# A filter's odd-frequency interpolation, started by half a channel in place of a whole one

## The chip, the cores and the metric

The kernel runs on one NeuronCore of a Trainium2 chip. The core has five engines that each work through their own list of instructions: TensorE (matrix products), VectorE, ScalarE and GpSimd (element by element), and SyncE, which here mostly issues DMA transfers, in order ("SP" in the profile). They meet through semaphores. Sixteen DMA engines move data between HBM and the core's memory. The metric is the time on the device, in microseconds: the median of three runs. In single precision a product of 128 x 512 takes more than one pass, so the profile shows several matmul instructions for one in the code.

## The reference, cut to what matters

Two layers; the change lies in the filter of the first. `x` is (4, 512, 512, 16): four images, 16 channels in, 16 out.

```python
def _L0_conv_ref(x, h0, numerators, denumerator):
    l1, l2 = 512, 512
    a = jnp.pad(denumerator, ((0, 0), (0, 0), (1, 0), (1, 0)), constant_values=1.0)
    b = jnp.pad(numerators, ((0, 0), (0, 0), (0, 0), (1, 0), (1, 0)), constant_values=0.0)
    H_truncated = jnp.fft.rfft2(b, s=(l1, l2)) / jnp.fft.rfft2(a, s=(l1, l2))
    h_truncated = jnp.fft.irfft2(H_truncated, s=(l1, l2))
    H_full = h0 + jnp.fft.rfft2(h_truncated, s=(2 * l1, 2 * l2))[0]
    X = jnp.fft.rfft2(x, s=(2 * l1, 2 * l2), axes=(-3, -2))
    Y = jnp.einsum('...hwi,ijhw->...hwj', X, H_full)
    return jnp.fft.irfft2(Y, s=(2 * l1, 2 * l2), axes=(-3, -2))[..., :l1, :l2, :]

x = x + _L0_conv_ref(_gn(x), L0_conv_h0, L0_conv_numerators, L0_conv_denumerator)
x = x + _L1_conv_ref(_gn(x), L1_conv_kernel, L1_conv_bias, L1_conv_radius)
```

For each pair of an input and an output channel, the filter is a quotient of two polynomials at 512 x 512 frequencies. It is brought back to 512 x 512 taps and transformed again at twice the length, so it is needed at the old frequencies along the second axis (the even ones of the long transform) and at those between them (the odd ones).

## The kernel before, in words

Four stages follow one another: the filter, the forward transform of the images, the product with the filter and the way back along one axis, and the last stage with the second layer. TensorE runs a stage's instructions after those of the stage before it. The change lies in the filter stage, `filter_phase`.

**The pairs.** The list `work` holds 512 entries: output channel `j` (16), half `kp` of the first axis's frequencies (2), half `h` of the even second-axis frequencies (2), and two input channels `i`, `i + 1` (8 steps). For a channel that is 32 entries, 16 for each `kp`. An entry goes through three passes of the main loop (line 490), so one pass works on three entries at different stages: `polynomials` (line 357, TensorE) evaluates numerator and denominator; `evict`, `products`, `terms` and `quotient` divide on ScalarE, VectorE and GpSimd (lines 368 to 393; the reciprocal is line 392); `taps` (line 410, TensorE) goes back along the first axis and `placed` (line 421, ScalarE) puts the outcome into the staged tiles `st`. With the last entry of a `(j, kp, h)` four DMAs (line 428) store the tiles into `g_d[h]`: two halves `a` of the 128 rows, and in each two groups `q` of 16 rows, at row 64 a + 32 q + 16 kp. A half `kp` therefore fills four groups of 16 rows, and columns that belong to channel `j` alone.

**The interpolation.** `odd(j)` makes the odd frequencies of channel `j` from the even ones: 16 blocks `tb`, each of four rows in two places. A block is loaded by four DMAs of 256 KB (`ev_in`, line 448; two buffers, the next block is asked for one block ahead), multiplied by the constant `todd` (line 462), copied by ScalarE to `ot` (line 467), and stored by four DMAs of 256 KB into `g_d[2]` and `g_d[3]` (line 468). It is a generator: it yields four times in a block, after the two products that fill one PSUM tile. What lies between two yields is called a unit here. A channel has 64 units, the kernel 1024.

**How the two are interleaved.** `odds()` runs through the channels and holds each back until `done[0]` has reached 64 (j + 1) + 8; `done[0]` grows by 2 with each finished entry of `work`. A pass of the loop asks the generator twice (lines 493 and 506), so at most two units run in a pass. After the loop, line 521 adds 8 and what is left of the interpolation runs on its own (line 522), with nothing beside it.

**The order.** `InOrder` fixes the order of the instructions of TensorE, VectorE, ScalarE and GpSimd inside the loop to that of the program. SyncE's list of DMAs isn't fixed in this way: its order is made by the framework's planner from what is ready. The queue itself works in order, so a DMA that waits holds back those behind it. The statistics of the images for the next stage run in the same loop on VectorE (`beside`, line 586).

Of the kernel before, what the change touches and what calls it, by code (L numbers as in the profile page):

```python
# [49 lines left out]
C = 16  # L50
# [150 lines left out]
def dram(t, row, offset, *dims):  # L201

    pitch = t.shape[1]
    lead = [[pitch, t.shape[0]]] if row is None else []
    return bass.AP(tensor=t.tensor, offset=t.offset + (row or 0) * pitch + offset,
                   ap=lead + [list(d) for d in dims])
# [28 lines left out]
def filter_phase(tc, cst, h0, num, den, g_d, beside):  # L235
    nc = tc.nc
    with ExitStack() as ctx:
# [193 lines left out]
                            in_=st[a].rearrange("p (q r e) i -> p q r (e i)", q=2, e=8)[:, q],  # L431
                        )

        def odd(j):

            def place(tb):
                first = ((0, 96), (64, 32))[tb // 8]
                return [(first[c] + 4 * (tb % 8)) * GP + j * 8 * C for c in range(2)]  # L440

            step = [GP, 4], [1, 8 * C]

            def load(tb):
                ev = evp.tile([P, 2, 2, 32 * C], F32, name="ev_in")
                for h in range(2):
                    for c in range(2):
                        nc.sync.dma_start(
                            out=ev[:, h, c].rearrange("p (s e) -> p s e", s=4),
                            in_=dram(g_d[h], None, place(tb)[c], *step),  # L450
                        )
                return ev

            ev = load(0)
            for tb in range(16):
                after = load(tb + 1) if tb < 15 else None
                for hh in range(2):
                    ot = odp.tile([P, 2, 32 * C], F32, name=f"ot{hh}")
                    for c in range(2):
                        pt = ps_t.tile([P, 32 * C], F32, name="pt", tag="t")  # L460
                        for kc in range(2):
                            nc.tensor.matmul(  # L462
                                pt, todd[:, c, kc, hh * P : hh * P + P], ev[:, kc, c],
                                start=(kc == 0), stop=(kc == 1),
                            )
                        yield
                        nc.scalar.copy(ot[:, c], pt)
                        nc.sync.dma_start(
                            out=dram(g_d[2 + hh], None, place(tb)[c], *step),
                            in_=ot[:, c].rearrange("p (s e) -> p s e", s=4),  # L470
                        )
                ev = after

        def odds():

            for j in range(C):
                while done[0] < 64 * (j + 1) + 8:
                    yield
                yield from odd(j)

        work = [dict(j=j, h=h, i=i, kp=kp)
                for j in range(C) for kp in range(2) for h in range(2) for i in range(0, C, 2)]
        done, us = [0], {}
        order = InOrder(tc, nc.tensor, nc.vector, nc.scalar, nc.gpsimd)
        rest = odds()
        for _ in weights(0):
            pass
        quad(0, 0, 0)
        coming = iter(())
        for p in range(len(work) + 2):  # L490
            new, mid, last = (work[p - k] if 0 <= p - k < len(work) else None for k in range(3))
            with order:
# [18 lines left out]
                j, kp, r = p // 32, p // 16 % 2, p % 16  # L511
# [952 lines left out]
```

## Time and profile before

| | |
|---|---|
| time before, median of three runs | 16199.08 us (16192.73 to 16224.64) |
| the profiled execution's own time | 16219.56 us |
| its span, first to last instruction | 16217.8 us |
| filter stage, to the end of line 462 | about 3776 us |
| of it, line 462 on TensorE | 4096 instructions, 1924.9 us busy, from 291.0 us on |
| line 392, reciprocal on VectorE | 1024 instructions, 1722.9 us busy |
| mean granted TensorE clock | 0.969 of full speed |

The span is one execution, a little slower than the median of the runs; shares and durations are read from it. Busy time of TensorE is modelled: matmuls overlap in the array, so the time from one start to the next is a better measure of what one costs than its mean duration. A share of busy time is only told for the stretch that it was taken over, since the stages have different limits. In an order of time, a figure in brackets is idle time of the engine before the instruction, with what ended it.

### The profile page before, as it was taken

How to read it: one execution, taken by the hardware profiler on the slowest of the kernel's cores; microseconds unless marked ns; L12 is line 12 of the kernel's file. 1: busy time of each engine (PE TensorE's matmuls, PEld its weight loads, DVE VectorE, ACT ScalarE, POOL GpSimd, SP SyncE). 2: the span in 40 equal slices, each digit the busy share in tenths (PEclk: the TensorE clock that was granted, in tenths of full speed). 3: DMA queues.
4: the chain of work that ended last, by engine and by line, in shares of the span. 5: the costliest groups of instructions: out<-in, count | busy, mean ns of one | idle time of the engine just before them, and what ended most of it. 6: DMA issues, size and time to landing. Idle time of an engine off the chain costs nothing. (4 is left out here: it accounts for less than half of the span.)

```text
span 16217.8 us, 539020 instructions
## 1 busy us (share of the span) xinstructions
PE 14720.9 (91%) x232588; PEld 10874.5 (67%) x232588; DVE 10679.6 (66%) x21019; ACT 8839.0 (55%) x17007; POOL 10556.5 (65%) x10157
## 2 busy tenths in 40 slices
PE   7999999999988888888888888888888889888898
PEld 5555555554557666667676676677676767777787
DVE  8999999993545555555555555555555555778877
ACT  4666666663345555555555555555555553147788
POOL 7777777772356666666666666666666665667766
PEclk8999999999999999999999999999999999989899
DMA  4888888888878888888888888888888888975521
GB/s 138 239 244 246 244 245 239 244 242 259 251 271 329 326 330 329 330 329 326 329 327 328 330 327 329 326 324 330 329 329 330 328 330 305 326 253 196 197 103 66
DMA packets 2917339, 4542.72 MB, mean 280 GB/s; under 512 B 125730, under 2 KB 2094076, under 8 KB 2805262
## 3 DMA queue, kind: packets, MB, share of 16 engines
q1 hardware_dynamic: 2705758, 3836.11, 68.6%
q0 software_dynamic: 172336, 605.00, 9.4%
q10 hardware_dynamic: 36864, 67.13, 1.2%
q8 instruction: 1830, 29.98, 0.7%
q14 instruction: 551, 4.51, 0.1%
HBM read 3030.45 MB, written 1477.31 MB: 278 GB/s over the span
## 5 line engine op out<-in xcount | busy, mean ns | idle before, releaser
L848 PEld LDWEIGHTS pm<-xe,gh 128*32 128x32 f32 x131328 | 1996.9, 111 | 1437.8 <-issue 1141.2
L848 PE MATMUL pm<-xe,gh 128*32 128x64 f32 x131328 | 2366.9, 222 | 649.6 <-issue 320.2
L832 PE MATMUL pg<-c_dg,g 64*128 64x128 f32 x32832 | 2607.1, 290 | 311.9 <-ACT gh L732 195.8
L877 DVE TENSOR_TENSOR z<-zq,pz 128x256 f32<-128x256 f32 x2052 | 860.0, 419 | 2956.7 <-ACT zq L876 2952.5
L832 PEld LDWEIGHTS pg<-c_dg,g 64*128 64x128 f32 x32832 | 2143.6, 191 | 575.4 <-ACT gh L732 245.2
L732 ACT COPY gh<-pg 128x512 f32<-128x512 f32 x2567 | 1447.8, 585 | 1302.8 <-PE pg L832 1299.9
L462 PE MATMUL pt<-ev_in,c_todd 128*128 128x512 f32 x4096 | 1924.9, 609 | 9.1 <-DMA ev_in<-g_d 9.0
L392 DVE RECIPROCAL dn<-dn 128x256 f32<-128x256 f32 x1024 | 1722.9, 1724 | 17.6
L393 POOL TENSOR_TENSOR sp<-m,dn 128x512 f32<-128x512 f32 x1024 | 1301.4, 1271 | 592.0 <-DVE dn L392 555.2
L812 ACT COPY xe<-xl 64x1024 f32<-64x1024 f32 x513 | 539.0, 1051 | 1868.9 <-POOL xl L803 1868.9
L730 DVE COPY gh<-pg 128x512 f32<-128x512 f32 x1537 | 1055.4, 687 | 661.0 <-PE pg L832 658.4
L869 PE MATMUL pz<-c_ident,yf 128*128 128x128 f32 x8208 | 1378.5, 291 | 18.5 <-issue 11.6
L801 POOL TENSOR_TENSOR xu<-xe,c_late 128x256 f32<-128x256 f32 x2052 | 1374.5, 694 | 21.7 <-DVE xe L730 6.9
L462 PEld LDWEIGHTS pt<-ev_in,c_todd 128*128 128x128 f32 x4096 | 729.1, 190 | 909.9 <-issue 772.9
L421 ACT COPY st<-pg 128x256 f32<-128x256 f32 x2048 | 617.0, 390 | 1300.9 <-PE pg L410 1300.9
L410 PEld LDWEIGHTS pg<-c_dinv,sp 64*128 64x128 f32 x16384 | 1005.5, 196 | 442.1 <-ACT sp L398 232.6
L803 POOL TENSOR_TENSOR xl<-xl,xu 128x1024 f32<-128x1024 f32 x513 | 1209.2, 2357 | 40.2
L1307 PE MATMUL pc<-l_band,xn 128*128 128x160 f32 (+2 forms) x6144 | 1112.8, 341 | 70.7 <-DVE e_o L1362 70.1
L410 PE MATMUL pg<-c_dinv,sp 64*128 64x128 f32 x16384 | 1108.1, 287 | 60.3 <-ACT sp L398 44.6
L885 POOL TENSOR_TENSOR zd<-z 128x512 f32<-128x512 f32 x513 | 654.5, 1276 | 778.8 <-DVE z L877 778.8
L917 POOL DMA_DIRECT2D y_d<-yo x511 | 296.5, 580 | 1275.9 <-ACT yo L732 1250.3
L906 PE MATMUL py<-z,c_ig 128*64 128x256 f32 x6156 | 1120.5, 396 | 6.5 <-issue 2.7
(216 smaller groups left out, 30900.2 us busy)
## 6 DMA issues: line engine op xcount, KB each, us to landing
xe<-xf_d SPq DMA_DIRECT2D x1026, 1536.0 KB
g<-g_d SPq DMA_DIRECT2D x511, 1024.0 KB
g_d<-st SPq DMA_DIRECT2D x256, 1024.0 KB
ev_in<-g_d SPq DMA_DIRECT2D x1024, 256.0 KB
g_d<-ot SPq DMA_DIRECT2D x1024, 256.0 KB
xf_d<-xe POOLq DMA_DIRECT2D x513, 448.0 KB, 8.2
xf_d<-xl POOLq DMA_DIRECT2D x513, 448.0 KB, 6.3
x_d<-xo SPq DMA_DIRECT2D x128, 1024.0 KB
```

What stands on the lines that cost most here:

```text
L392: nc.vector.reciprocal(dn, dn)
L393: nc.gpsimd.tensor_mul(w["sp"][:, v], w["m"][:, v], bc(dn, 2, [P, 2, 2, P]))
L410: nc.tensor.matmul(pg[u][:, n, k].rearrange("p a x -> p (a x)"), w["sp"][q, n, k, c, :], dinv[q, 2 * kp + k, c, :], start=(c == 0), stop=( ...
L462: nc.tensor.matmul(pt, todd[:, c, kc, hh * P : hh * P + P], ev[:, kc, c], start=(kc == 0), stop=(kc == 1),)
L732: nc.scalar.copy(dst, src)
L801: nc.gpsimd.tensor_mul(u[:, :, h, c], xe[:, :, h, 1 - c], bc(late[:, 1 + c], 2, [P, F, 2]))
L803: nc.gpsimd.tensor_add(xl.rearrange("p f h c k -> p (f h c k)"), xl.rearrange("p f h c k -> p (f h c k)"), u.rearrange("p f h c k -> p (f ...
L832: nc.tensor.matmul(pg[c][:, j % 4], g[half, j], dg[half], start=True, stop=True)
L848: nc.tensor.matmul(pm[32 * q : 32 * q + 32, g % 8], gh[:, f].rearrange("p c j -> p (c j)"), xe[:, :, f].rearrange("p t h c k -> p t (h c k ...
L869: nc.tensor.transpose(pz[:, t % 4].rearrange("p v q x -> p (v q x)"), y[:, at].rearrange("p g x -> p (g x)"), ident)
L906: nc.tensor.matmul(py[64 * half : 64 * half + 64, odd], ig[:, s0, c2], zs.rearrange("p (t h) j -> p h t j", h=2), start=(c2 == 0), stop=(c ...
L1307: nc.tensor.matmul(pc[:, lo:hi, :].rearrange("p w j -> p (w j)"), xns[q][:, h * P + dh : h * P + dh + P], bands[dh][:, o : o + hi - lo, :] ...
```

## The change

`odd` gets a second argument `kp` and makes only the eight blocks whose rows belong to this half: 4 kp to 4 kp + 3 and 8 + 4 kp to 8 + 4 kp + 3. `odds()` goes through 32 halves in place of 16 channels, and holds half `n` back until `done[0]` has reached 32 (n + 1) + 8. The work inside a block is as it was.

```diff
-        def odd(j):
+        def odd(j, kp):
...
-            ev = load(0)
-            for tb in range(16):
-                after = load(tb + 1) if tb < 15 else None
+            tbs = [8 * c + 4 * kp + t for c in range(2) for t in range(4)]
+            ev = load(tbs[0])
+            for n, tb in enumerate(tbs):
+                after = load(tbs[n + 1]) if n < 7 else None
                 for hh in range(2):
                     ot = odp.tile([P, 2, 32 * C], F32, name=f"ot{hh}")
...
         def odds():
 
-            for j in range(C):
-                while done[0] < 64 * (j + 1) + 8:
+            for n in range(2 * C):
+                while done[0] < 32 * (n + 1) + 8:
                     yield
-                yield from odd(j)
+                yield from odd(n // 2, n % 2)
```

## The prediction, made before the changed kernel was built

> **What bounds the kernel around the change.** I started with the busy shares by stretches of time. The filter stage ends at 3776 us: there the interpolation's last matmul (line 462) stops and the next stage's first group statistics start. I cut it where the order of work changes: line 462 runs nowhere before 291.0 us, runs between the pairs until 3640, and runs alone after that. Columns of the first view: stretch and its length, then busy us with (instructions) of TensorE, its weight loads, VectorE, ScalarE and GpSimd, then the granted TensorE clock, the DMA share and GB/s (an engine with nothing to do shows 0.00).
>
> ```profile
> 176.00:291.00 115.00, 89.09 (x853) 70.96 (x850) 106.80 (x90) 56.50 (x128) 83.75 (x67) 0.68 0.30 92
> 291.00:403.00 112.00, 112.00 (x924) 64.89 (x920) 103.10 (x97) 69.64 (x154) 83.36 (x75) 0.98 0.78 231
> 403.00:515.00 112.00, 112.00 (x963) 65.69 (x962) 106.14 (x97) 70.19 (x156) 81.74 (x66) 1.00 0.82 243
> 3640.00:3776.00 136.00, 126.76 (x288) 54.79 (x288) 0.00 (x0) 43.22 (x77) 0.00 (x0) 0.96 1.01 297
> ```
>
> Each of the first three rows holds 16 pairs (the product of line 377 was counted 16 times in each). So 16 pairs take 115 us without interpolation and 112 us with it. Without it VectorE is busy 93% of the time and TensorE 77%, at a granted clock of only 0.68. With it TensorE is busy throughout and sets the pace, 7.0 us a pair, and VectorE follows at 95%. In the last row the pairs are over: VectorE and GpSimd do nothing, and what is left is interpolation alone.
>
> Then I read TensorE's own order of time over that last stretch (start us, duration, line, operation, shape, count, and in brackets the idle time and what ended it):
>
> ```profile
> 3639.82 14.13 PE L462 MATMUL pt<-ev_in,c_todd 128*128 128x512 f32 x32
> ...
> 3662.72 24.13 PE L462 MATMUL pt<-ev_in,c_todd 128*128 128x512 f32 x50 [8.77 <-DMA ev_in<-g_d]
> ...
> 3687.10 88.77 PE L462 MATMUL pt<-ev_in,c_todd 128*128 128x512 f32 x206 [0.25 <-DMA ev_in<-g_d]
> ```
>
> The records are 32 + 50 + 206 = 288. A unit (what runs between two yields) leaves 4 of them, since all 1024 units leave 4096. So this tail is 72 units: 8 left over from channel 14, and the 64 of channel 15. Once it runs evenly, a unit takes 88.77 / (206 / 4) = 1.724 us. There is one gap of some 9 us, at the start of channel 15.
>
> **The change part by part.**
>
> *The tail gets shorter.* The interpolation now starts after 32 evaluated frequencies and a lag of 8, and does 32 units, in place of 64 and 64. The generator is asked twice per loop pass and does one unit each time. So a half of 32 units takes 16 passes, exactly one half's worth of pairs: the halves follow one another without a hole, as the channels do now. When the pairs end, the same 8 units are left over, and then 32 instead of 64: 40 units in place of 72. The 32 that leave the tail belong to its even part: 32 x 1.724 = **55.2 us less**. The gap of 9 us stays: the first loads of the last half stand behind the last stored tile and the full output buffers as now.
>
> Here a rule of the Trainium skill weighs in. "DMA: Bandwidth & Descriptors", section "Bandwidth", puts the limit of HBM for one core at about 358 GB/s. If transfers set the tail, its pace by that figure would be: a block of 4 units reads 4 x 256 KB and writes 4 x 256 KB, 2.10 MB, so 8 blocks are 16.8 MB, 47 us by the rule (an estimate). The row of the tail shows 297 GB/s with the DMA engines at 1.01, gap included, which makes 56 us. TensorE's row gives 55.2. The transfers are as close to the edge as the matmuls, but both shrink by the same 32 units, so I take the trace's 55.2; by the rule the gain would be 8 us smaller.
>
> *The first channel's second half gets company.* The 32 units that leave the tail appear beside 16 pairs that had none: from 176 us, 16 pairs before the first start at 291, to 291. Their cost is the difference of two rows, 112 - 115 = **-3 us**, because TensorE had 26 us idle there and worked at clock 0.68. The row 291 to 403 is the proper one: it contains such a start from a slow clock. Bounds: -3 us if the clock rises as it did at 291. If it stayed at 0.68, TensorE's 89.1 us and 32 x 1.724 / 0.68 = 81.1 us would add up to 170 us, +55. I take -3: the granted clock is 0.98 in the very row in which the units begin. ScalarE's extra 32 copies of 0.6 us (19 us) lie in its idle time (56.5 of 115 us busy), and the DMA goes from 0.30 to the 0.78 of the next row.
>
> *Each half start now reads what was just stored.* This speaks against the change. Before, a channel's first blocks read rows of its first half, stored more than 16 passes earlier; the rows of the second half are wanted only at the fifth block. Now every half's first loads need the store of its last 16 frequencies, made 4 passes earlier. The loads go through SP's queue in order, and behind a waiting load stand the stores of finished output tiles and the next loads; ScalarE's copy waits for those output buffers, and TensorE for the loads. The dependency itself doesn't widen: the blocks of half kp (0 to 3 and 8 to 11, or 4 to 7 and 12 to 15) cover exactly the 16 rows at 16 kp in each group of 32 that this half stored.
>
> What does such a wait cost? The trace has two at the start of the run, where SP reached loads right behind the stores (line, what it waited for: total us, times, longest):
>
> ```profile
> SPq L448 <- DMA g_d<-st: 4.1, 2, 2.1
> ```
>
> So a store is read back 2.1 us after its last issue. Where SP would reach the load now shows in its own order of time at a channel boundary. The store of the last 16 frequencies is issued here, and channel 4 takes its first block into the buffer that frees at 1180 us:
>
> ```profile
> 1164.76 10.51 SPq L428 DMA_DIRECT2D g_d<-st  x4
> 1175.37 5.26 SPq L468 DMA_DIRECT2D g_d<-ot  x4
> 1180.72 2.85 SPq L448 DMA_DIRECT2D ev_in<-g_d  x4
> ```
>
> From the last store's issue (1175.3) to the load are 5.4 us, more than 2.1. And the block is first used at 1193.93, in the matmuls of the fifth pass after the one that stored (TensorE's order of time): 10 us after the load's issue ends at 1183.57. A wait of a few us on SP is therefore covered; the output tiles have two buffers of each kind as cover for the stores behind it. The skill's rule is harder: "DMA: Bandwidth & Descriptors", section "Anatomy of one DMA — SWDGE (gpsimd) path", says that the semaphore wait is made on the issuing sequencer, with about 2 us fixed for completion and a "surprisingly long delay" when HBM is written. Charged at each of the 31 half starts that lie beside pairs, 2 us are 62 us, which would eat the whole gain. By the row it is 0, bounds 0 and 31 x 2.1 = 65 us. I take 0, because the load comes 5.4 us after the store and is needed 10 us after it.
>
> *The order of blocks* (0 to 3, 8 to 11, then 4 to 7, 12 to 15) changes no size and no count: 0, with nothing to bound it below.
>
> **The sum.** -55.2 - 3 + 0 = -58 us. Against the profiled execution, whose own time is 16219.6 us (span 16217.8), that is 16161, or -0.36%. The same on the median of the runs, 16199.1, gives **16141 us**. Later stages start 58 us earlier and have nothing that the filter's inner order could change.
>
> **Rivals.**
>
> A. *As summed*: 16141, chance 0.74; its own range is 16112 to 16166 (the gap at the last half's start could double, +9; the load waits could leak a little; 3 runs spread over 32 us).
>
> B. *The cover isn't free*: the clock stays low for the 16 early pairs (+55 in place of -3), or load waits of 1 to 2 us leak through at each half start. Gain and price cancel: 16199. For it: clock 0.68 there. Against it: 0.98 as soon as the units run. Chance 0.13.
>
> C. *Half starts stall TensorE* (slower): the just stored rows are late under load, SP holds the first loads, and TensorE, whose order is written out by hand, stands still. The nearest row is the one stall of this sort, the gap before 3662.72, about 9 us from idle 8.77. At each of 31 half starts: 272 us, 16141 + 272 = 16413. It decides from 58 / 31 = 1.9 us a half start on. For it: SP's queue is in order, and the DMA is at 0.82. Against it: 10 us of cover, and that gap came when 8 units had run without pairs between them. Chance 0.13.
>
> That the change doesn't do what it says is excluded by the count of passes above: 40 units must remain.
>
> **How the numbers follow.** A measurement of this kernel tells about 0.2% (32 us) from no change. Faster by more than that is A, 0.74; within it B, 0.13; slower C, 0.13. The range reaches from A's lower end to the middle of B, 16112 to 16200: A nearly whole and about half of B make 0.8.
>
> **What would show it.** In the changed profile line 462 begins near 176 us and not 291; the stretch from there has TensorE full, clock near 1 and 16 pairs in 112 us; after the last pair come about 160 records of line 462 in some 81 us; the next stage's first matmul comes near 3718 in place of 3776. SP's waits of line 448 on the stored tile say how much the half starts cost: more than a few us each, and with TensorE waiting for ev_in between 300 and 3600 us, and C is right. A first half beside the pairs at a clock well under 1 would be B.

## The result, and the profile after

| | before | after |
|---|---|---|
| median of seven runs | 16202.4 us (16191.7 to 16224.6) | 16161.2 us (16142.0 to 16167.6) |
| ratio of the times, with its 95% interval | | 0.9969 (0.9958 to 0.998) |
| span of the profiled execution | 16217.8 us | 16159.4 us |
| first product of the interpolation | 291.0 us | 178.0 us |
| last pair done, tail begins | 3639.8 us | 3638.7 us |
| next stage's first matmul | 3776.5 us | 3720.7 us |
| next stage's first transposition of image data | 3793.2 us | 3736.6 us |

By the ratio the kernel is faster by 0.31%, with an interval from 0.20% to 0.42%: 32 to 68 us. The medians themselves differ by 41 us, 0.25%. The two profiled executions differ by 58.4 us, and 55.9 us of that (3776.5 - 3720.7, before rounding) lie in the filter stage.

First the busy shares of the changed kernel by stretches (stretch, length, busy us with instructions of TensorE, weight loads, VectorE, ScalarE and GpSimd, then clock, DMA share and GB/s):

```profile
60.00:176.00 116.00, 87.67 (x842) 71.10 (x840) 107.01 (x101) 56.29 (x127) 86.55 (x77) 0.69 0.36 110
176.00:288.00 112.00, 112.00 (x929) 64.93 (x928) 102.23 (x87) 69.91 (x155) 80.02 (x64) 0.98 0.77 228
288.00:400.00 112.00, 112.00 (x966) 66.14 (x964) 105.57 (x99) 69.97 (x156) 85.52 (x76) 1.00 0.84 247
```

The row from 176 to 288 now looks as the row 291 to 403 did before: TensorE full, clock 0.98, and VectorE about as busy as it was there (102 of 112 us; 107 of 115 from 176 to 291 us before). The switch from a slow to a full clock has moved 113 us forward.

Then TensorE's order of time at the end of the filter stage of the changed kernel:

```profile
3638.72 14.13 PE L463 MATMUL pt<-ev_in,c_todd 128*128 128x512 f32 x32
3661.86 37.76 PE L463 MATMUL pt<-ev_in,c_todd 128*128 128x512 f32 x82 [9.02 <-DMA ev_in<-g_d]
3699.98 20.01 PE L463 MATMUL pt<-ev_in,c_todd 128*128 128x512 f32 x46 [0.36 <-DMA ev_in<-g_d]
3720.67 0.39 PE L543 MATMUL gn_ps<-gn_mu,c_mean 128*128 128x8 f32 x2 [0.68 <-ACT ot L468]
```

32 + 82 + 46 = 160 records, 40 units where there were 72. The idle gap of 9 us is still there. From the first record of the tail to the next stage it is 81.95 us, and it was 136.7 us.

And SyncE's waits of the changed kernel (line, what it waited for: total us, times, longest), where a price at the half starts would show:

```profile
SPq L448 <- DMA g_d<-st: 4.1, 2, 2.1
```

It is the same line as before the change: two waits, and none of the 31 half starts beside pairs added one. TensorE's own waits for `ev_in` between 300 and 3600 us are no longer than 0.3 us each.

### The profile page after: what moved, and what is told of

It reads as the page before. It is cut to its first block, busy times and chain, and to the rows that moved or that the text cites. A ratio compares the mean times of both kernels' runs of the same rounds, so it can differ in the third digit from the quotient of the medians.

```text
span 16159.4 us, 538992 instructions
## 1 busy us (share of the span) xinstructions
PE 14688.7 (91%) x232588; PEld 10845.3 (67%) x232588; DVE 10687.8 (66%) x21019; ACT 8828.2 (55%) x17007; POOL 10568.8 (65%) x10157
## 5 line engine op out<-in xcount | busy, mean ns | idle before, releaser
L870 PE MATMUL pz<-c_ident,yf 128*128 128x128 f32 x8208 | 1375.2, 290 | 16.6 <-issue 11.1
L410 PE MATMUL pg<-c_dinv,sp 64*128 64x128 f32 x16384 | 1083.6, 283 | 36.3 <-ACT sp L398 26.8
```

The costliest lines, as they stand in the source:

```text
L410: nc.tensor.matmul(pg[u][:, n, k].rearrange("p a x -> p (a x)"), w["sp"][q, n, k, c, :], dinv[q, 2 * kp + k, c, :], start=(c == 0), stop=( ...
L870: nc.tensor.transpose(pz[:, t % 4].rearrange("p v q x -> p (v q x)"), y[:, at].rearrange("p g x -> p (g x)"), ident)
```

## The experiments

In all of them the places in the trace are compared, since the later stages, whose code is the same in every kernel, differ between executions: the product stage alone, from its first output store to its last, took between 8816.5 and 8850.7 us in the ten profiled executions of this study. Each experiment was executed once.

**e1_late_start: the new order of blocks without the early start.**

```diff
-                while done[0] < 32 * (n + 1) + 8:
+                while done[0] < 64 * (n // 2 + 1) + 8:
```

> Halves in their new order of blocks, but started when the whole channel is there, as before the change. My theory (the early start alone makes the gain, by moving 32 units out of the tail): the interpolation begins near 291 us, the tail after the last pair has 72 units again and ends near 3776 us, time near 16200. The rival (the new order of blocks or of SyncE's transfers brings something by itself): the end lies well before 3776 us.

Measured: first product at 293.1 us, tail from 3641.9, next stage at 3778.7 us, time 16218 us (16200 for the kernel before on the same chip). Its tail, in TensorE's order of time:

```profile
3641.86 14.13 PE L463 MATMUL pt<-ev_in,c_todd 128*128 128x512 f32 x32
3665.16 37.35 PE L463 MATMUL pt<-ev_in,c_todd 128*128 128x512 f32 x82 [9.18 <-DMA ev_in<-g_d]
3702.74 75.28 PE L463 MATMUL pt<-ev_in,c_todd 128*128 128x512 f32 x174 [0.23 <-DMA ev_in<-g_d]
3778.70 0.39 PE L543 MATMUL gn_ps<-gn_mu,c_mean 128*128 128x8 f32 x2 [0.68 <-ACT ot L468]
```

The 288 records of before are back, and with them the whole time: the tail takes 136.8 us, and took 136.7. (Its times are some 2 us later than before, but that offset is there at the 17th pair already, whose first reciprocal comes at 146.8 us and came at 144.6: long ahead of any difference in the order of work.) The order of blocks brings nothing by itself.

**e5_no_first: are the moved units free?** Loads, products and copies of the first half are left out; zeros are stored in their place, so one thirty-second of the odd frequencies is not computed.

```diff
+            if (j, kp) == (0, 0):
+                zero = odp.tile([P, 2, 32 * C], F32, name="ot0")[:, 0]
+                nc.gpsimd.memset(zero, 0.0)
...
+                            yield
+                            nc.sync.dma_start(
+                                out=dram(g_d[2 + hh], None, place(tb)[c], *step),
+                                in_=zero.rearrange("p (s e) -> p s e", s=4),
+                            )
+                return
             ev = load(tbs[0])
```

> The first half's interpolation is left out but for its stores, which store zeros: 32 units of loads, products and copies beside the first channel's second half are gone. My theory (they were free there): the pairs end where they end in the changed kernel, at 3639 us, or up to 3 us later because TensorE's clock stays low until 290 us. The rival (units beside pairs cost their full price): 55 us earlier.

Measured, in the shares by stretches of this kernel:

```profile
176.00:288.00 112.00, 86.18 (x852) 69.66 (x853) 106.62 (x90) 55.46 (x126) 82.97 (x67) 0.70 0.62 189
288.00:400.00 112.00, 112.00 (x933) 65.19 (x926) 102.61 (x98) 69.40 (x155) 83.24 (x75) 0.98 0.77 227
```

Without the 32 units TensorE has 26 us idle again and its clock is back at 0.70, yet nothing moves: the pairs end at 3638.2 us (3638.7 in the changed kernel) and the next stage starts at 3720.5 (3720.7). The units cost nothing there in sum. They also don't save anything: the 3 us that I had credited to the row don't show. This kernel differs from the changed one in two things at once, the missing units and the place where TensorE comes out of its low clock, 16 pairs later; what each is worth is read from pair to pair further down.

**e6_no_last: what do the same units cost in the tail?** The same edit with `(j, kp) == (C - 1, 1)`: the last half is not computed, its stores write zeros.

> The last half's interpolation is left out but for its stores, which store zeros: 32 units of loads, products and copies in the tail are gone. My theory (a unit in the tail costs its full 1.72 us of TensorE): the tail keeps 8 units (14 us) and then only transfers, a last stored tile of 4.2 MB and 32 stores of 256 KB, together 12.6 MB or some 40 us at 300 GB/s; the next stage's first matmul comes 35 to 65 us before 3721 us. The rival (the tail's length is set elsewhere, by the stores): less than 15 us earlier.

Measured: the next stage's first matmul at 3657.5 us, 63 us earlier. That matmul belongs to statistics that need no transfer. The first transposition that needs image data comes at 3699.0 us where it came at 3736.6: only 37.6 us earlier, and the first output store of the product stage moves by about as much (4608.1 us; 4644.5 in the changed kernel). Shares of this kernel in the stretch between:

```profile
3638.00:3698.00 60.00, 20.61 (x80) 11.34 (x76) 5.38 (x29) 8.63 (x18) 1.68 (x2) 0.67 1.12 361
```

TensorE is idle for most of the 60 us, and the DMA engines move 361 GB/s. So the 32 units, with the gap of 9 us before them, take 63 us from TensorE's order, but without them the tail is a queue of transfers that doesn't shrink as much. The rival (stores alone set the length, under 15 us) is out.

**e7_half_product: matmuls or transfers?** In the last half one of the two products of each unit is left out (half of the sum), all transfers stay.

```diff
+            ks = 1 if (j, kp) == (C - 1, 1) else 2
...
-                        for kc in range(2):
+                        for kc in range(ks):
```

> In the last half only one of the two products of a unit is made (the sum over the other half of the even frequencies is left out), so TensorE's work for these 32 units falls from 55 to 27.5 us, while all loads and stores stay. If TensorE sets the tail's pace: the next stage's first matmul comes 20 to 27 us earlier than 3721 us. If the transfers set it (last stored tile and 40 units make 25 MB, 84 us at 300 GB/s): less than 8 us earlier.

Measured: next stage at 3712.3 us, 8.4 us earlier, at the edge of what I had given for transfers and far from the 20 us and more of TensorE alone. In TensorE's order of time the products now stand still for 2 to 2.7 us in four of the six blocks shown, until the loaded block is there; below them are the shares of a stretch of this tail:

```profile
3675.66 2.90 PE L464 MATMUL pt<-ev_in,c_todd 128*128 128x512 f32 x6 [2.06 <-DMA ev_in<-g_d]
3680.99 5.37 PE L464 MATMUL pt<-ev_in,c_todd 128*128 128x512 f32 x8 [2.43 <-DMA ev_in<-g_d]
3687.05 3.76 PE L464 MATMUL pt<-ev_in,c_todd 128*128 128x512 f32 x8 [0.69 <-ACT ot L469]
3693.49 1.10 PE L464 MATMUL pt<-ev_in,c_todd 128*128 128x512 f32 x2 [2.67 <-DMA ev_in<-g_d]
3695.22 4.36 PE L464 MATMUL pt<-ev_in,c_todd 128*128 128x512 f32 x6 [0.64 <-ACT ot L469]
3701.82 5.41 PE L464 MATMUL pt<-ev_in,c_todd 128*128 128x512 f32 x8 [2.24 <-DMA ev_in<-g_d]
3707.89 3.75 PE L464 MATMUL pt<-ev_in,c_todd 128*128 128x512 f32 x8 [0.66 <-ACT ot L469]
```

```profile
3676.00:3708.00 32.00, 22.66 (x39) 7.95 (x38) 0.00 (x0) 11.12 (x19) 0.00 (x0) 0.84 1.08 320
```

A block is 8 records here. From 3680.99 to 3707.89 there are four, 6.1 to 8.3 us each and 6.7 us on the mean. The row agrees: at its 320 GB/s, with the DMA share at 1.08, the 2.097 MB of a block take 6.55 us. A block's matmuls in the changed kernel take 4 x 1.724 = 6.9 us, and there TensorE is busy nearly all the time, at a smaller DMA share (the same columns, the changed kernel):

```profile
3664.00:3720.00 56.00, 55.63 (x126) 23.93 (x125) 0.00 (x0) 18.17 (x31) 0.00 (x0) 0.98 0.92 267
```

So TensorE sets the even part of the changed kernel's tail, with the transfers 3 to 5% behind.

**e4_lag24, e8_lag6, e2_lag4, e3_lag0: how much cover has a half start?** One number is changed, the lag (the cut shows lag 4); for 24 the 8 added after the loop becomes 24 as well.

```diff
-                while done[0] < 32 * (n + 1) + 8:
+                while done[0] < 32 * (n + 1) + 4:
```

> Lag 24 in place of 8: every half starts 8 passes later. My theory (each unit pushed into the tail costs its 1.72 us, and cover beyond lag 8 brings nothing): 16 units more in the tail (56), the next stage's first matmul 27.6 us later, near 3748 us, pairs' end as before within 1 us. The rival (the half starts at lag 8 still cost something): the pairs end earlier than at lag 8, by more than 3 us.

> Lag 6: one pass (6.7 us) less of cover. My theory: lag 8 has some 10 us of cover from the load's issue to its use, so 3 us or more are left; no waits of TensorE for ev_in between 300 and 3600 us beyond the 60 us of the changed kernel; the tail has 38 units, and the next stage's first matmul comes 3 us earlier, near 3717 us. The rival (half starts at lag 8 are on the edge): waits at most half starts, later than 3721 us.

> Lag 4 in place of 8: two passes (13.4 us) less between a half's last store and its first products. Lag 0 cost 16.6 us at each half start (pairs end 513.8 us later, over 31). My theory (a fixed chain of store, read back and load of some 30 us, covered by the passes between): 16.6 - 13.4 = about 3 us of wait at each half start, some 100 us, time near 16255; the tail has 36 units. The rival (the wait at lag 0 comes from the planner's order of SyncE's transfers in that kernel, not from the chain's length): no waits, filter stage 7 us shorter than at lag 8.

> The lag of 8 behind each half's last store is taken to 0, so a half's first products come half a pass after its last store is issued in place of four and a half passes. My theory (the lag is what covers the store and the read back): store issue 8 to 10 us, 2 us to be read back, load 3 us and some 2 us to land make 15 to 17 us, less half a pass (3.5 us): TensorE waits 12 us or more for ev_in at each of 31 half starts, some 370 us, time near 16520; the tail would be 8 units shorter (14 us). The rival (the queues hide the store in any case): no waits, time near 16147.

| lag | passes from store to first product | tail begins | next stage | time, one run |
|---|---|---|---|---|
| 24 | 12.5 | 3640.1 us | 3747.4 us | 16182 us |
| 8 (the change) | 4.5 | 3638.7 us | 3720.7 us | 16161 us |
| 6 | 3.5 | 3637.9 us | 3719.2 us | 16163 us |
| 4 | 2.5 | 3740.6 us | 3818.0 us | 16236 us |
| 0 | 0.5 | 4152.5 us | 4226.3 us | 16658 us |

Between 24 and 8 the pairs end within 1.4 us of each other, and 16 units more in the tail cost 26.8 us (before rounding), 1.67 us each. One pass less (6) is still free. Two passes less (4) make 101.9 us, 3.3 us at each of 31 half starts, and at lag 0 it is 513.8 us, 16.6 us at each. In lag 0, TensorE's order of time at a half start:

```profile
1050.13 2.06 PE L410 MATMUL pg<-c_dinv,sp 64*128 64x128 f32 x32
...
1053.19 1.13 PE L463 MATMUL pt<-ev_in,c_todd 128*128 128x512 f32 x2
1068.24 4.26 PE L463 MATMUL pt<-ev_in,c_todd 128*128 128x512 f32 x6 [13.92 <-DMA ev_in<-g_d]
1072.43 2.06 PE L410 MATMUL pg<-c_dinv,sp 64*128 64x128 f32 x32
```

and SyncE's order beside it:

```profile
1053.17 8.13 SPq L428 DMA_DIRECT2D g_d<-st  x4
1061.39 2.65 SPq L469 DMA_DIRECT2D g_d<-ot  x1
1064.14 3.54 SPq L448 DMA_DIRECT2D ev_in<-g_d  x4
```

The waits of TensorE in lag 0 and in lag 4 for the loaded block (engine, line, what it waited for: total us, times, longest):

```profile
PE pt L463 <- DMA ev_in<-g_d: 408.2, 29, 14.9
```

```profile
PE pt L463 <- DMA ev_in<-g_d: 60.0, 28, 2.7
```

The chain is seen whole in SyncE's lines: 8.1 us to issue the stored tile, one store of an output tile, then the rest of the load, issued 1064 to 1068 us, and TensorE goes on at 1068.2. From the store to TensorE's next product are 15 us, not the 30 that I had put into the expectation of lag 4; what was right in it is the difference of 13.4 us for two passes. SyncE itself waits for the stored tile no longer than 2.0 us at a time even there (48.9 us in 33 waits); the long part is the store's own issue. My 12 us or more for a half start at lag 0 fell short as well: TensorE waits 408.2 / 29 = 14 us, and the pairs lose 16.6. The rest isn't taken apart; part of it is that the six matmuls after the gap take 0.71 us each (4.26 / 6), where 8 between pairs take 3.70 us. The rival for lag 0 (the queues hide it) and the one for lag 4 (no waits) are both out.

No kernel here that does the whole work is faster than the changed one by a measurable amount: lag 6 gains 1.5 us of filter stage, and its one run is 2 us longer.

## Why the prediction was right

**Tail, -55.2 us: right in size.** The tail went from 136.7 to 81.95 us, 54.8 us less, with 32 units gone as counted. That TensorE's pace was the proper price is shown by the changed kernel's row (55.6 of 56 us busy) and by e7: the limit of transfers lies at 6.55 to 6.7 us a block, and so only a little below TensorE's 6.9. An estimate from the Trainium skill's figure for HBM ("DMA: Bandwidth & Descriptors", section "Bandwidth") had it at 5.86 us (2.097 MB at 358 GB/s), and for the 32 units about 8 us short; this mix of loads and stores moved 320 GB/s. What I said of the two being close was true, which also means that a faster matmul there would gain little: 8.4 us for half of the last half's matmuls.

**Beside the pairs, -3 us: mis-sized, and its sign came out by luck.** The two rows that I subtracted, 115 and 112 us, were cut at the interpolation's first product, so their edges lie at different places within a pair. Here are the same stretches from pair to pair: the first reciprocals of the 17th, the 33rd and the 49th pair (line 392 on VectorE), before and then in the changed kernel.

```profile
144.61 3.37 DVE L392 RECIPROCAL dn<-dn 128x256 f32<-128x256 f32 x2
258.01 3.37 DVE L392 RECIPROCAL dn<-dn 128x256 f32<-128x256 f32 x2
373.87 3.37 DVE L392 RECIPROCAL dn<-dn 128x256 f32<-128x256 f32 x2
```

```profile
144.26 3.37 DVE L392 RECIPROCAL dn<-dn 128x256 f32<-128x256 f32 x2
259.26 3.37 DVE L392 RECIPROCAL dn<-dn 128x256 f32<-128x256 f32 x2
372.72 3.37 DVE L392 RECIPROCAL dn<-dn 128x256 f32<-128x256 f32 x2
```

Before, 16 pairs without interpolation take 113.4 us, and the next 16, in which it starts, take 115.9: more, not less. In the changed kernel the start lies in the first 16, which take 115.0, and the next 16 take 113.5. So the moved units add 1.6 us, the next 16 pairs give 2.4 back, and the sum is -0.8 us. In e5, by the same pairs, it is 0.3 us more than in the changed kernel. That the units are nearly free there has its reason in VectorE: in e5 it is busy for 107 of the 112 us and waits for others for 4.6 us in all, while TensorE is busy for 86. The part that mattered, that the units are not charged a second time, is shown by e5.

**Half starts, 0 us: right; the 10 us of cover agree in part by luck.** One pass less (6.7 us) is free and two (13.4 us) are not, so the cover at lag 8 lies between these. Taken from the loss of the pairs it is 13.4 - 3.3 = 10.1 us by lag 4 and 26.8 - 16.6 = 10.2 by lag 0. But TensorE's waits alone (2.1 us each at lag 4, 14 at lag 0) would make it 11.3 and 12.7. And my 10 us, from the end of the load's issue to its use, left out what the load needs to land. Lag 4 shows that at a half start, SyncE's line first, then TensorE's:

```profile
1088.99 2.22 SPq L448 DMA_DIRECT2D ev_in<-g_d  x2
```

```profile
1093.70 2.84 PE L463 MATMUL pt<-ev_in,c_todd 128*128 128x512 f32 x6 [2.58 <-DMA ev_in<-g_d]
```

The issue ends at 1091.2 and TensorE goes on at 1093.7, 2.5 us later. By that reading some 8 of my 10 us were cover. The planner's order differs as well: from the second half on, some of a half's first loads go out ahead of the store at lags 4 and 0, and none does at lags 8 and 6. What the runs settle is that the cover is more than one pass and less than two.

The 2 us that the Trainium skill gives as fixed ("DMA: Bandwidth & Descriptors", section "Anatomy of one DMA — SWDGE (gpsimd) path") would have charged 62 us. That section is on transfers issued by GpSimd, and these are SyncE's. SyncE's waits for the stored tile are at most of that length (2.1 us at lags 8, 4 and 0); at lag 8 there are two, both at the start of the run, at lag 4 there are 32 (25.6 us in all) and at lag 0 there are 33. So the size fits, but charging it at every half start was wrong, and the order of time showed it: the wait is covered.

**The whole, -58 us.** The profiled executions differ by 58.4 us, and that this meets the sum so closely is luck: 55.9 us of it lie in the filter stage, and the remaining 2.5 us lie in stages that didn't change and are within what these differ by themselves. They fill the place of the -3 us, of which 1.1 came. The medians differ by 41 us, and the time of 16161 us lies 20 us above the forecast of 16141. The interval of the ratio, 32 to 68 us, contains both; the study can't tell 41 from 58. With the product stage alone varying by 34 us between executions, medians of a few runs could tell a step of this size from none but not measure it well; the filter stage's own end did that.

Rival C, the slower side, was a true mechanism that the chosen lag keeps away: it starts between lag 6 and lag 4. Its price at the nearest row (8.8 us a half) lay between what lags 4 and 0 cost.

## What to carry to other kernels

When background work lags behind the work that feeds it, its last portion runs alone at the end: its size is the granularity plus the lag, and halving the granularity is worth half a portion at the pace of the tail, provided that the place it moves to has an idle engine. Finer portions read fresher data, so read the cover in the order of time, from the load's landing to its first use, and try a shorter lag: here one pass less (6.7 us) was free, and two less cost 102 us in all. Compare stretches from one instance of an instruction to a later one, and not by windows whose edges fall anywhere: a difference of 3 us in 115 was made by the edges. And before a tail is priced by its busy engine, see how far behind the next limit is: it caps any later gain from making that engine faster.

## What the runs showed of the hardware

What the DMA engines moved depended on the mix, at busy shares that were above 1 each time. Stores alone, SBUF to HBM, ran at 346 GB/s (e6, 3644 to 3680 us), and the next stage's loads, nearly alone, at 418 GB/s (e6, 3684 to 3698 us). Alternating loads and stores of 256 KB made 320 GB/s in e7's tail, with half of TensorE's work in the last half out of the way.

Pairs at a low granted clock were no slower than pairs with interpolation at full clock: 16 of them took 113.4 us before (clock 0.68 from 176 to 291 us) and 113.5 us in the changed kernel (clock 0.98 to 1.00 from 176 to 400 us). VectorE was the busiest engine in the first case and TensorE in the second, so this is no price of the clock by itself. TensorE's own work does take longer at the low clock: the 32 products of line 410 took 3.78 us just before the interpolation's start at 178 us and 2.06 us right after it, and the first two units 5.43 us where later ones take 3.70.
